# A grouped expert FFN with one list of 143 slot tiles, its tokens in parts of 16 and 16 tiles, and two more gate groups inside the second attention

## The chip, the cores and the metric

The kernel runs on one core of one Trainium2 chip. The metric is device time in microseconds (us). The core has five engines with queues of their own: PE multiplies matrices (its weight loads are shown as PEld), DVE and ACT do element work, POOL does element work and issues the indirect DMAs, and SP issues the plain DMAs.

## The reference

A transformer block works on 8 x 512 tokens of width 256 in float32:

```python
x = x + 0.5 * _L0_ffn_ref(_layernorm(x), ...)      # expert choice: 8 experts take 1024 tokens each
x = x + _L0_attn_ref(_layernorm(x), ...)           # causal, 16 heads of 16
x = x + 0.5 * _L0_ffn_ref(_layernorm(x), ...)
x = x + 0.5 * _L1_ffn_ref(_layernorm(x), ...)      # "FFN one" below
x = x + _L1_attn_ref(_layernorm(x), ...)           # 16 heads of 64: "the second attention"
x = x + 0.5 * _L1_ffn_ref(_layernorm(x), ...)      # "FFN two" below
```

The change is in the last three lines. In `_L1_ffn_ref` every token goes to 4 of 16 experts, and to a shared expert:

```python
scores = softmax(x @ gate_w.T)                     # 4 groups of 4 experts; the best 2 groups stay
_, indices = lax.top_k(masked, 4); weights = take(scores, indices)
h1 = einsum('td,edi->tei', x, w1); h3 = einsum('td,edi->tei', x, w3)
y = einsum('tei,eid,te->td', silu(h1) * h3, w2, c) # c holds the weights; 256 -> 128 -> 256 per expert
z = silu(x @ ws1) * (x @ ws3) @ ws2                # shared expert, inner width 256
return y + z
```

## The kernel before

The residual `x` stays on the chip as 32 tiles of 128 tokens; a group is 4 tiles. The engine queues are filled in the order in which the Python code emits (`manual_schedule`), so a waiting instruction holds up everything behind it on its engine.

**The grouped FFN** (`Grouped`, from L1220) sorts token rows by expert through DRAM. For each part of the tokens there is a list of slots, cut into slot tiles of 128 rows of which each belongs to one expert. `routing` (L1264) computes the gate on DVE for all tiles of a part: softmax, the best groups, the four best experts by repeated maxima, then with a few matmuls and scans the slot of every token (`self.slot`), the expert that owns each slot tile (`self.owner`) and the weights (`self.coef`). It is a generator: `advance(steps, n)` runs it n pieces further. `send` (L1245) copies each normalised row to its four slots with four indirect DMAs per token tile, issued by POOL; one is issued only when the one before the previous has landed (two in flight). `tile_steps` (L1498) works through the slot tiles two at a time, as a pipeline over steps: `turn` transposes a pair loaded by `load` four steps earlier, `hide` (L1532) is the first matmul and the silu two steps later, `back` a transpose, `give` (L1555) the second matmul and the write to `ys_d`. A load of a part waits for all sends of that part. `gather` (L1352) fetches the four result rows of each token of a tile with four indirect DMAs, again with a limited number in flight (`flying`), into one of two `yg` buffers, and `add` (L1366) adds them to `x`, weighted, on DVE. `collect` (L1374) lists steps "add tile t - 2, gather tile t", which the caller places between other work. `shared` (L1452) is the shared expert as units of PE and DVE work that a `Pump` deals out.

**Two parts.** `PARTS` is 12 and 20 tiles. Each part has a slot list of its own, of `slot_tiles(t)` tiles: 63 for 12 token tiles and 95 for 20, the most that 16 experts with a last tile filled in part can need. That makes 158 slot tiles in each FFN, worked in 80 pairs.

**FFN one** (`ffn1_before`, L1608) takes the parts in the order 12, 20. It normalises the first three groups, routes them beside units of the shared expert, sends their rows, then normalises and routes the other five groups beside more units, sends those rows, empties the pump, and runs the tile steps. Part 0's results are collected within the steps from step 37 on, one tile in three steps; at step 37 the 4 MB of attention weights are also loaded (`attn1_weights`, L894). Part 1's 20 tiles are collected inside the attention.

**The second attention** (`_attn1`, L912) is a loop over 64 chunks of two heads, of two halves each. Lists of small pieces are put between: the gathers of FFN one, layernorm statistics, and `Front` (from L1700), which computes the gate logits of FFN two for the groups whose tokens are finished (five groups, 20 tiles), routes them (from chunk 47 on) and sends their rows.

**FFN two** (`ffn1_after`, L1751) has the parts 20, 12. It loads the expert weights, normalises the last three groups and computes their logits on PE, then runs the tile steps with the routing of part 1 inside (four pieces a step), then the sends of part 1. Part 0 is collected in two steps of three from step 53 on, two gathers in flight. After the steps come the 48 units of the shared expert; every second unit is followed by one collect step of part 1, with four gathers in flight. `out` is written tile by tile.

Of the kernel before, what the change touches and what calls it, by code (L numbers as in the profile page):

```python
# [45 lines left out]
PARTS = 12, 20  # L46
# [9 lines left out]


def slot_tiles(t):

    return (t * P * TOPK + E1 * (P - 1)) // P  # L60


class Kernel:
    def __init__(self, ctx, tc, w):
# [59 lines left out]
        self.slots_d, self.ys_d = {}, {}  # L124
        for t in PARTS:
            self.slots_d[t] = self.dram.tile([slot_tiles(t) * P, D], F32, name=f"slots_d{t}")
            self.ys_d[t] = self.dram.tile([slot_tiles(t) * P, D], F32, name=f"ys_d{t}")

    def clear(self, zero, part, parts):

        for t in PARTS:
            rows = self.slots_d[t].rearrange("(j p) d -> p j d", p=P)
            a, b = slot_tiles(t) * part // parts, slot_tiles(t) * (part + 1) // parts
            self.nc.sync.dma_start(out=rows[:, a:b, :], in_=bc(zero, 1, b - a))
# [777 lines left out]
    def _attn1(self, ctx, weights, one, after):  # L912
# [185 lines left out]
        turned, sends = [], list(range(a))  # L1098
        flags = {"routed": False}
# [4 lines left out]
        def listed(n):  # L1104
            b, c = divmod(n, NC)
            got = gathered(n - 1) if 1 <= n <= one.parts[1] + 2 else []
            if c == 0:
                ranges = []
                if b == 0:
                    ranges.append((self.stats1, QT, 2 * QT))  # L1110
                elif 2 <= b < B - 1:
                    got += [each(means, self.stats1, (b + 1) * QT + i) for i in range(0, QT, 2)]
                    ranges.append((self.stats1, (b + 1) * QT, QT))
# [7 lines left out]
            if (b, c) == (groups, 4):  # L1121
                got += [each(means, after.stats, (b - 1) * QT + i) for i in range(0, QT, 2)]
                got += roots([(after.stats, (b - 1) * QT, QT)])
            return got

        def fill(n, half):
            b, c = divmod(n, NC)
            if half == 0:
# [3 lines left out]
                if c == 3 and 2 <= b <= groups or (b, c) == (groups, 6):  # L1132
                    got += turned.pop(0)
# [20 lines left out]
        for g in range(2 * N + 1):  # L1154
# [20 lines left out]
            if n < N:  # L1175
                scores(n, half)
                if half == 1 and (c == 2 and 2 <= b <= groups or (b, c) == (groups, 5)):
# [19 lines left out]
    def topk(self, pool, vals, n, k, hots):  # L1197
# [6 lines left out]
        for r in range(k):  # L1204
# [3 lines left out]
            rank = pool.tile([P, T, n], F32, name=f"rank{n}")  # L1208
# [11 lines left out]
class Grouped:  # L1220


    def __init__(self, k, n, parts):
        self.k, self.n, self.parts = k, n, parts
        self.base = (0, parts[0])
        self.tiles = [slot_tiles(t) for t in parts]
        self.slots_d = [k.slots_d[t] for t in parts]
        self.ys_d = [k.ys_d[t] for t in parts]
        late, most = k.late, max(parts)
# [4 lines left out]
        self.owner = [late.tile([1, slot_tiles(most)], I32, name=f"owner{h}") for h in range(2)]  # L1234
        self.stats = k.ln_tiles(late)
        self.sent, self.of_part = [], ([], [])
# [8 lines left out]
    def send(self, h, t, row):  # L1245

        nc, tc = self.k.nc, self.k.tc
        key = f"slots{self.n}{h}"
        for r in range(TOPK):
            inst = nc.gpsimd.indirect_dma_start(  # L1250
                out=self.slots_d[h][:, :],
                out_offset=bass.IndirectOffsetOnAxis(ap=self.slot[h][:, r, t : t + 1], axis=0),
                in_=row, in_offset=None,
                bounds_check=self.tiles[h] * P - 1, oob_is_err=True,
# [4 lines left out]
            tc.declare_no_dep(inst, group=key, keep=before, reason="slots of one part are all different")  # L1259
# [4 lines left out]
    def routing(self, h, lg, pool, row_psum):  # L1264
# [49 lines left out]
        tiles_i = pool.tile([P, E1], I32, name="tiles_i")  # L1314
        nc.vector.tensor_scalar(tiles_i, inc[:, :, HT - 1], float(P - 1), None, ALU.add)
        nc.vector.tensor_scalar(tiles_i, tiles_i, 7, None, ALU.arith_shift_right)
        nc.vector.tensor_tensor(inc.rearrange(flat), inc.rearrange(flat), pb, ALU.subtract)
        pa = row_psum(E1 * HT)
        nc.tensor.matmul(pa, lhsT=k.tri, rhs=chosen.rearrange(flat), start=True, stop=True)
        tiles = pool.tile([P, E1], F32, name="tiles")  # L1320
        nc.vector.tensor_copy(tiles, tiles_i)
        upto = pool.tile([P, E1], F32, name="upto")
        nc.vector.tensor_tensor_scan(upto, k.ones[:, 0:E1], tiles, 0.0, ALU.mult, ALU.add)
        base = pool.tile([P, E1], F32, name="base")
        nc.vector.tensor_tensor(base, upto, tiles, ALU.subtract)
        nc.vector.tensor_scalar(base, base, float(P), None, ALU.mult)
        nc.vector.tensor_tensor(inc.rearrange(flat), inc.rearrange(flat), pa, ALU.add)
        yield
        nc.vector.tensor_tensor(inc, inc, bc(base, 2, HT), ALU.add)
# [11 lines left out]
        past = pool.tile([P, E1], F32, name="past")  # L1341
        number = pool.tile([P, 1], F32, name="number")
        nc.vector.tensor_scalar(past, upto, k.lanes[:, 0:1], None, ALU.is_le, ALU.add, accum_out=number)  # L1343
# [8 lines left out]
    def gather(self, h, t, flying):  # L1352

        nc, tc = self.k.nc, self.k.tc
        y = self.y[h, t] = self.k.late.tile([P, TOPK, D], F32, name="yg", bufs=2)
        for r in range(TOPK):
            inst = nc.gpsimd.indirect_dma_start(  # L1357
                out=y[:, r, :], out_offset=None, in_=self.ys_d[h][:, :],
                in_offset=bass.IndirectOffsetOnAxis(ap=self.slot[h][:, r, t : t + 1], axis=0),
                bounds_check=self.tiles[h] * P - 1, oob_is_err=True,  # L1360
            ).ins
            for other in self.got[-flying : 1 - flying]:
                tc.add_manual_dep(inst, other.name, SYNC, reason="few transfers at a time")
            self.got.append(inst)

    def add(self, h, t, ranks=range(TOPK)):  # L1366
        at = self.base[h] + t
        x = self.k.x[:, at, :]
        for r in ranks:
            self.k.nc.vector.scalar_tensor_tensor(  # L1370
                x, self.y[h, t][:, r, :], self.coef[h][:, r, t : t + 1], x, ALU.mult, ALU.add
            )

    def collect(self, h, flying, then=None):  # L1374

        def step(t):
            def run():
                if t >= 2:
                    self.add(h, t - 2)
                    if then is not None:  # L1380
                        then(self.base[h] + t - 2)
                if t < self.parts[h]:
                    self.gather(h, t, flying)
            return run
        return [step(t) for t in range(self.parts[h] + 2)]
# [66 lines left out]
    def shared(self, g):  # L1452
# [4 lines left out]
        def hidden(s):  # L1457
# [14 lines left out]

            def dve():
# [4 lines left out]
        def outputs(i):  # L1478
# [11 lines left out]

            def dve():
# [6 lines left out]
    def tile_steps(self):  # L1498
# [3 lines left out]
        where = [(h, i, min(2, self.tiles[h] - i)) for h in range(2) for i in range(0, self.tiles[h], 2)]  # L1502
        st = [{} for _ in where]

# [410 lines left out]
```

## Time and profile before

| what | value |
|---|---|
| median of 3 runs | 4050.3 us (4047.67 to 4058.88) |
| the profiled execution | 4017.39 us, span 4015.7 us, mean granted PE clock 0.936 |
| FFN one: x has landed, first slot tile on PE, last result row of a slot tile | 1859.0, 2029.2, 2309.8 us |
| second attention: first transpose of it, last projection added to x | 2310.6, 3561.1 us |
| FFN two: first slot tile, first unit of the shared expert, end | 3581.1, 3895.7, 4015.7 us |
| PE, DVE, ACT, POOL busy, share of the span | 91%, 46%, 36%, 30% |

The times in the table are starts of instructions in the timeline of the profiled execution, in us from the start of the span. In the profile, L12 is line 12 of the kernel before; "x1264" is a number of instructions; "<-" after the bar names what ended most of the idle time before a group. In a table of windows the columns are the window, its length, the busy time of PE, PEld, DVE, ACT and POOL with the number of instructions, the granted PE clock, the busy share of the DMA engines and GB/s.

### The profile page before, as it was taken

The numbers are of one execution on the slowest core, as the hardware profiler recorded it, in microseconds if no ns is written. First come the engines' busy times: TensorE is split into PE (matmuls) and PEld (weight loads), VectorE is DVE, ScalarE is ACT, GpSimd is POOL, SyncE is SP. The second block draws the span as 40 slices with busy tenths as digits, with TensorE's granted clock in tenths as the row PEclk, the third lists the DMA queues.
The fourth block names the chain that finished last, engine by engine and source line by source line (L and its number), as shares of the span: only waits on it lengthen the run. The fifth ranks groups of instructions, "written<-read, shape, count | busy, mean of one in ns | idle before, by whom it ended". The sixth has DMA issues, their size and how long they took to land.

```text
span 4015.7 us, 52125 instructions
## 1 busy us (share of the span) xinstructions
PE 3662.2 (91%) x18444; PEld 2343.5 (58%) x18444; DVE 1858.5 (46%) x4396; ACT 1432.8 (36%) x2849; POOL 1203.8 (30%) x1074
## 2 busy tenths in 40 slices
PE   5799995999997599997798999999999999989978
PEld 5466662555556366665487845555555554558855
DVE  5312206555553421213733556666556576554444
ACT  2122221444443122222122355555455554533311
POOL 2233335334322133331553322220000004504254
PEclk6899997999986599998899999999999999989989
DMA  8533322010103033324256600110000001136543
GB/s 271 161 73 75 73 30 80 17 27 17 28 22 106 18 77 71 70 52 123 78 198 218 188 28 27 30 29 1 1 1 1 1 1 48 58 108 218 182 147 105
DMA packets 256141, 306.99 MB, mean 76 GB/s; under 512 B 34320, under 2 KB 225936, under 8 KB 255632
## 3 DMA queue, kind: packets, MB, share of 16 engines
q1 hardware_dynamic: 206736, 202.43, 15.8%
q0 software_dynamic: 49152, 101.24, 10.5%
q8 instruction: 153, 2.51, 0.3%
q14 instruction: 100, 0.82, 0.1%
HBM read 161.48 MB, written 133.69 MB: 74 GB/s over the span
## 4 chain that ended last, share of the span: by engine, by line
PE 41%; issue 4%; DVE 3%; DMA 3%; POOL 3%; ACT 1%; POOLq 0%; DVEq 0%; ACTq 0%; SPq 0%
PE sp L986 6%; PE tp L1006 6%; PE zp L1033 6%; PE pq L964 6%; PE hs L1537 4%; PE yp L1048 3%; PE pv L953 3%; PE yps L1559 2%; POOL slots_d L1250 2%; DMA yg<-ys_d,slot 2%; PE hp L1464 2%; POOL yg L1357 1%; PE tpx L1523 1%; DMA acc_d<-ob,idx 1%; PE rp L1020 1%
## 5 line engine op out<-in xcount | busy, mean ns | idle before, releaser
L478 PE MATMUL hp<-exT,w 128*128 128x512 f32 x1024 | 453.4, 597 | 0.0
L492 PE MATMUL op<-w,hid 128*128 128x256 f32 x2048 | 451.9, 380 | 0.0
L995 ACT ACTIVATE ex<-sp,nmax 128x512 f32<-128x512 f32 x512 | 344.7, 685 | 242.3 <-DVE nmax L992 242.3
L492 PEld LDWEIGHTS op<-w,hid 128*128 128x128 f32 x2048 | 387.7, 190 | 64.3 <-issue 15.3
L1357 POOL DMA_INDIRECT yg<-ys_d,slot x256 | 266.0, 1039 | 510.2 <-DVE x L1370 296.2
L497 DVE TENSOR_TENSOR ob<-op,b 128x256 f32<-128x256 f32 x128 | 54.4, 425 | 647.4 <-PE op L492 572.0
L731 DVE CUSTOM_DVE_ANT_0 junk<-sp,mask 128x128 f32<-128x128 f32 (+3 forms) x512 | 251.1, 490 | 198.0 <-PE sp L722 174.3
L499 POOL DMA_INDIRECT acc_d<-ob,idx x128 | 207.1, 1618 | 439.8 <-ACT ob L498 193.0
L992 DVE TENSOR_REDUCE nmax<-sp 128x2 f32<-128x1024 f32 x256 | 301.7, 1220 | 80.3 <-PE sp L986 80.2
L478 PEld LDWEIGHTS hp<-exT,w 128*128 128x128 f32 x1024 | 193.5, 191 | 219.9 <-issue 216.9
L1006 PEld LDWEIGHTS tp<-ident,ex 128*128 128x128 f32 x2048 | 234.4, 141 | 147.4 <-issue 86.6
L1537 PE MATMUL hs<-w_sb,xT 128*128 x1264 | 310.4, 390 | 2.5 <-DMA xs<-slots_d 1.3
L482 ACT ACTIVATE hid<-hp,b 128x512 f32<-128x512 f32 x256 | 175.9, 687 | 342.3 <-PE hp L478 342.3
L1006 PE MATMUL tp<-ident,ex 128*128 128x128 f32 x2048 | 272.5, 275 | 6.7 <-ACT ex L995 5.4
L1537 PEld LDWEIGHTS hs<-w_sb,xT 128*128 128x128 f32 x1264 | 248.4, 197 | 39.2 <-ACT xT L195 2.7
L1250 POOL DMA_INDIRECT slots_d<-wide,slot x176 | 174.4, 991 | 318.3 <-DVE past L1343 144.3
L986 PE MATMUL sp<-qk,qk 64*128 64x512 f32 x1024 | 254.4, 615 | 0.0
L964 PE MATMUL pq<-xnT,wide 128*128 128x512 f32 x512 | 247.5, 607 | 1.2 <-ACT xnT L195 0.8
L197 DVE COPY eT<-tp 128x512 f32<-128x512 f32 x256 | 176.9, 691 | 140.7 <-PE tp L1006 139.9
L1033 PE MATMUL zp<-eT,v 128*64 128x512 f32 x1024 | 236.0, 603 | 0.0
L195 ACT COPY eT<-tp 128x512 f32<-128x512 f32 x256 | 149.5, 584 | 240.4 <-PE tp L1006 240.4
L449 POOL DMA_INDIRECT ex<-xn_d,idx x128 | 131.3, 1025 | 345.9 <-DVE idx L440 311.8
(298 smaller groups left out, 5512.3 us busy)
## 6 DMA issues: line engine op xcount, KB each, us to landing
xs<-slots_d SPq DMA_DIRECT2D x156, 256.0 KB, 2.8
ys_d<-ys SPq DMA_DIRECT2D x156, 256.0 KB, 2.5
w<-in_W SPq DMA_DIRECT2D x32, 1024.0 KB, 6.1
w_sb<-in_w SPq DMA_DIRECT2D x24, 512.0 KB, 6.5
slots_d<-zero SPq DMA_DIRECT2D x7, 1536.0 KB, 12.9
xn_d<-xn SPq DMA_DIRECT2D x16, 512.0 KB, 4.2
acc_d<-x SPq DMA_DIRECT2D x8, 1024.0 KB, 5.7
x<-acc_d SPq DMA_DIRECT2D x8, 1024.0 KB, 9.5
```

What stands on the lines that cost most here:

```text
L478: nc.tensor.matmul(hp, lhsT=w1[:, c, f * P : f * P + P], rhs=exT[e][:, c, h * CH : h * CH + CH], start=(c == 0), stop=(c == DC - 1),)
L492: nc.tensor.matmul(op, lhsT=hid[h][:, f, i * P : i * P + P], rhs=w2[:, f, :], start=(f == 0), stop=(f == FC - 1),)
L731: nc.vector.tensor_tensor_reduce(out=junk[:, :wd], in0=sps[h // 2][:, h % 2, at : at + wd], in1=mask[:, S - wd :], scale=1.0, scalar=NEG, ...
L964: nc.tensor.matmul(pp, lhsT=(wq, wk)[a][:, k, c * P : c * P + P], rhs=xnT[b][:, k, :], start=(k == 0), stop=(k == DC - 1),)
L986: nc.tensor.matmul(sp[:, j, :], lhsT=q[r, qt * P : qt * P + P], rhs=k[r, :], start=True, stop=True)
L992: nc.vector.tensor_reduce(nmax, sp, AX.X, ALU.max, negate=True)
L995: nc.scalar.activation(ex[:, j, :], sp[:, j, :], AF.Exp, bias=nmax[:, j : j + 1], accum_out=ch["sums"][:, qt, j : j + 1],)
L1006: nc.tensor.transpose(tp[:, k, :], ch["ex", qt][:, j, k * P : k * P + P], self.ident)
L1033: nc.tensor.matmul(zp[DK1 * j : DK1 * j + DK1, :], lhsT=v[b, h][:, k, at : at + DK1], rhs=ch["eT"][:, j, k, :], start=(k == 0), stop=(k == ...
L1250: inst = nc.gpsimd.indirect_dma_start(out=self.slots_d[h][:, :], out_offset=bass.IndirectOffsetOnAxis(ap=self.slot[h][:, r, t : t + 1], ax ...
L1357: inst = nc.gpsimd.indirect_dma_start(out=y[:, r, :], out_offset=None, in_=self.ys_d[h][:, :], in_offset=bass.IndirectOffsetOnAxis(ap=self ...
L1537: nc.tensor.matmul(hp[:, u].rearrange("p a i -> p (a i)"), lhsT=st[j]["xT"][:, u, c, :], rhs=self.w13[:, bass.ds(st[j]["e"][u], 1), c, :]. ...
```

## The change

One list of `SLOT_TILES` = 143 slot tiles per FFN takes the place of two lists. Part 0 fills whole slot tiles from the front, as many as each expert has; the rows of an expert that are left over go to one of 16 tail tiles, which part 1's rows fill up before they go on. With parts of 16 and 16 tiles, FFN one works on the first 48 tiles (`starts`, `tiles`) as soon as part 0's rows are sent, and on the other 95 after part 1's; part 0's results are complete after tile 80 (`whole`). FFN two keeps 20 and 12: 64 tiles, 79 tiles, 96.

```diff
-PARTS = 12, 20
+PARTS = (16, 16), (20, 12)
+SLOT_TILES = (NT * TOPK + E1 * (P - 1)) // P
...
+        first = TOPK * parts[0] - E1
+        self.starts, self.tiles = (0, first), (first, SLOT_TILES - first)
+        self.whole = TOPK * parts[0] + E1
```

`routing` gets more instructions. For part 0, on arrays of 16 to 64 columns except the last three:

```diff
+            nc.vector.tensor_copy(tiles_i, count)
+            nc.vector.tensor_scalar(tiles_i, tiles_i, 7, None, ALU.arith_shift_right)
...
+            nc.vector.tensor_tensor(over, count, shift, ALU.add)
+            nc.vector.tensor_scalar(tail, each, full, float(P), ALU.add, ALU.mult)
+            nc.vector.tensor_scalar(at, upto, float(P), None, ALU.mult)
+            nc.vector.tensor_tensor(jump, tail, at, ALU.subtract)
...
+        nc.vector.tensor_tensor(inc, inc, bc(shift, 2, HT), ALU.add)
+        nc.vector.scalar_tensor_tensor(beyond, inc, 0.0, bc(jump, 2, HT), ALU.is_ge, ALU.mult)
+        yield
+        nc.vector.tensor_tensor(inc, inc, bc(at, 2, HT), ALU.add)
+        nc.vector.tensor_tensor(inc, inc, beyond, ALU.add)
```

Loads of part 0, sends of part 1, gathers of part 0 and writes of results behind tile 80 (96) are declared independent of each other. The four loads at the border of the parts are issued in the step that turns the first of them, not four steps ahead:

```diff
         def turn(j):
+            if j == early:
+                for ahead in range(4):
+                    load(j + ahead)
...
-            load(j + 4)
+            if j >= early or j + 4 < early:
+                load(j + 4)
...
-        first = sum(h == 0 for h, _, _ in where)
-        return load, step, len(where) + 4, first
+        known = sum(self.starts[h] + i < self.whole for h, i, _ in where)
+        return load, step, len(where) + 4, known
```

`collect` and `gather` get a mode `more`: four tiles in flight instead of two, every second one in two of the four `xs` buffers.

```diff
+        if more and t % 2:
+            halves = [self.work.tile([P, 2, D], F32, name="xs", bufs=4) for _ in range(2)]
+            y = [halves[r // 2][:, r % 2, :] for r in range(TOPK)]
...
+        depth = 4 if more else 2
```

The prelude of FFN one is a stream: `Pump.beside` runs three pieces of a generator before each hidden unit of the shared expert, one before each output unit, and four where no unit is left. The first four groups are normalised and their logits computed at the start; the other four are inside the second stream.

```diff
+    def beside(self, steps):
+        more = True
+        while more:
+            more = advance(steps, self.units[0][0].steps if self.units else 4)
+            self.run(1)
...
+        f.normal(3)
+        f.columns(3)
+        for g in (2, 3):
+            f.logits(g, lg, g * QT)
...
+        pump.beside(f.routing(0, lg, f.route, f.row_psum))
         for t in range(a):
             f.send(0, t, f.xn[:, t, :])
...
+        def second():
+            for g in range(a // QT, TT // QT):
+                for i in range(0, QT, 2):
+                    for t in range(g * QT + i, g * QT + i + 2):
+                        k.ln_mean(f.route, f.stats, t)
+                    yield
+                y = k.ln_root(f.route, f.stats, g * QT, QT)
+                yield
+                k.ln_rest(f.route, f.stats, g * QT, QT, y)
+                yield
+                f.normal(g)
+                yield
+                f.columns(g)
+                f.logits(g, lg, g * QT - a)
+                pump.feed(groups[g][0])
+                if g > a // QT:
+                    pump.feed(groups[g - 1][1])
+                yield
+            pump.feed(groups[-1][1])
+            yield from f.routing(1, lg, f.route, f.row_psum)
+        pump.beside(second())
         for t in range(f.parts[1]):
             f.send(1, t, f.xn[:, a + t, :])
...
-        begin, weights = first + 5, None
+        begin, weights = known + 5, None
...
-            if i >= begin and (i - begin) % 3 == 0 and coming:
+            if i >= begin and (i - begin) % 5 % 2 == 0 and coming:
                 coming.pop(0)()
```

In the attention, statistics, transposes and logits of groups 5 and 6 (tiles 20 to 27) are added at chunks 52 to 54 and 60 to 63; their logits go to a buffer `lg1`, and the routing there still covers the first 20 tiles.

```diff
+        later = {groups: 6, groups + 1: 6, groups + 2: 7}
...
-            if (b, c) == (groups, 4):
+            if b >= groups and c == 4:
...
-                if half == 1 and (c == 2 and 2 <= b <= groups or (b, c) == (groups, 5)):
+                if half == 1 and (c == 2 and 2 <= b <= groups or b >= groups and c == later[b] - 1):
                     turned.append(front.units(b - 2 if c == 2 else b - 1, row_psum))
```

FFN two then has one group left to normalise and gate before its steps. The routing runs three pieces a step, with two of the other groups' normalisations in the first two steps; part 0 is collected in three steps of five, and the rest is spread over all 48 units, with two gathers in flight throughout.

```diff
-        for g in range(a // QT, TT // QT):
-            f.normal(g)
-            f.columns(g)
-            f.logits(g, lg, g * QT - a)
-        steps = f.routing(1, lg, f.route, f.row_psum)
+        g = TT // QT - 1
+        k.ln_range(f.route, f.stats, g * QT, QT)
+        f.normal(g)
+        f.columns(g)
...
+        steps = f.routing(1, f.lg1, f.route, f.row_psum)
...
-                sending = not advance(steps, 4)
+                sending = not advance(steps, 3)
+                if i < 2:
+                    f.normal(rest.pop(0))
...
-            if i >= begin and (i - begin) % 3 != 2 and early:
+            if i >= begin and (i - begin) % 5 % 2 == 0 and early:
                 early.pop(0)()
-        last = f.collect(1, 4, done)
+        last = f.collect(1, 2, done, more=True)
...
+        ends = early + last
+        pace, at = len(ends) / len(pump.units), 0
         while pump.units or pump.pending:
             pump.run(1)
             at += 1
-            if at % 2 == 0 and early:
-                early.pop(0)()
-            elif at % 2 == 0 and last:
-                last.pop(0)()
+            if ends and len(early + last) - len(ends) < at * pace:
+                ends.pop(0)()
```

## The prediction

> **What bounds the kernel now.** I read the table of windows first, to see where PE is full, then the timelines of PE, POOL and DVE around the gaps.
>
> ```profile
> 1900.00:1940.00 40.00, 25.50 (x70) 14.90 (x69) 35.18 (x117) 4.07 (x7) 16.25 (x17) 0.78 0.14 51
> 2500.00:2700.00 200.00, 199.60 (x970) 112.04 (x970) 127.96 (x207) 105.67 (x250) 47.76 (x45) 1.00 0.09 27
> 3650.00:3700.00 50.00, 50.00 (x281) 44.60 (x280) 19.48 (x40) 17.03 (x39) 25.59 (x27) 1.00 0.71 235
> 3800.00:3850.00 50.00, 40.14 (x170) 32.90 (x169) 22.36 (x49) 10.47 (x23) 28.03 (x26) 0.81 0.57 171
> 3900.00:3950.00 50.00, 36.60 (x107) 19.68 (x105) 23.72 (x50) 5.25 (x9) 34.16 (x33) 0.93 0.35 100
> ```
>
> PE sets the pace in the attention (199.6 of 200 us) and in undisturbed slot-tile steps (50 of 50). It doesn't in FFN one's prelude, where DVE does the routing (35.2 of 40), nor where results are gathered (40.1 and 36.6 of 50). PE's timeline gives the price of a step, the same instruction one pair later, 3.25 us, and the stall where FFN one passes to its second part:
>
> ```profile
> 3653.82 1.03 PE L1559 MATMUL yps<-w_sb,aT 128*128 x4
> 3657.07 1.03 PE L1559 MATMUL yps<-w_sb,aT 128*128 x4
> ...
> 2137.22 1.11 PE L1523 MATMUL tpx<-ident,xs 128*128 128x128 f32 x4 [6.55 <-DMA xs<-slots_d]
> ```
>
> What PE waits for at 2137 is on POOL:
>
> ```profile
> 1917.33 1.03 POOL L1250 DMA_INDIRECT slots_d<-wide,slot  x1 [66.29 <-PE hp L1464]
> 1984.15 0.99 POOL L1250 DMA_INDIRECT slots_d<-wide,slot  x1 [0.30 <-issue]
> 2002.11 0.98 POOL L1250 DMA_INDIRECT slots_d<-wide,slot  x1 [16.97 <-DVE past L1343]
> 2131.63 0.98 POOL L1250 DMA_INDIRECT slots_d<-wide,slot  x1 [0.41 <-DMA slots_d<-wide,slot]
> ```
>
> The first 48 sends take 66.8 us (1.42 each, two in flight). The 80 of part 1 wait for the second routing and take 129.5 us: 1.70 each beside the steps' own loads and writes, about 1.38 without. The load follows the last, and PE goes on 5.6 us after its issue. The gathers of FFN two are on POOL too:
>
> ```profile
> 3763.31 1.07 POOL L1357 DMA_INDIRECT yg<-ys_d,slot  x1 [65.78 <-DMA ys_d<-ys]
> 3906.57 1.02 POOL L1357 DMA_INDIRECT yg<-ys_d,slot  x1 [1.20 <-DVE x L1370]
> ...
> 3917.98 1.02 POOL L1357 DMA_INDIRECT yg<-ys_d,slot  x1 [0.30 <-issue]
> 3919.31 1.02 POOL L1357 DMA_INDIRECT yg<-ys_d,slot  x1 [0.30 <-issue]
> ...
> 3980.06 1.02 POOL L1357 DMA_INDIRECT yg<-ys_d,slot  x1 [0.31 <-issue]
> ```
>
> Between the first two lines lie 19 tiles of four gathers: 7.54 us a tile with two in flight. With four in flight they leave every 1.33 us, 5.3 a tile. So the steps from 53 on are bound by two-in-flight gathers, and the end by what is left on PE after 3984.
>
> **Change: the tiles removed.** 158 slot tiles become 143, 80 pairs 72: 8 steps x 3.25 = 26 us per FFN where PE sets the pace. Whether they count depends on the chain of sends and gathers, so I follow that chain.
>
> **FFN one.** Part 0's slots were ready at 1916.4. Ahead of them now stand a fourth group's 8 transposes (2.15 us here), 16 gate matmuls (3.4) and four more tiles of statistics on DVE (4 x 0.53): +7.5, since each stands on the path in turn. Routing took 34.2 us for 12 tiles (1882.2 to 1916.4) and 38.9 for 20 (1963.2 to 2002.1); 16 tiles, 36.5. New are 7 small DVE instructions at 0.2 and three on 256 columns at 0.43, +2.8. So 1882.2 + 7.5 + 39.3 = 1929. Now 64 sends at 1.42: 2020. The second routing (the first's 39 us, plus four groups' statistics, rows and gates, 43 us for five groups before, 1920 to 1963) ends about 2008, under these sends, and costs nothing; without that cover each us late is a us lost. Steps begin at 2020 + 5.6 = 2026, against 2029. Part 1's 64 sends: 5 at 1.4, 38 beside the steps at 1.70, 21 at 1.38 once no loads are left, 101 us: 2121, and step 24 goes on at 2127. PE reaches it at 2026 + 24 x 3.25 = 2104, so it waits 23 us. Step 32 went on at 2137 before: a gain of 10.
>
> From there both versions have 48 pairs on PE. Before, these ended at 2310 with gathers at leisure (one tile in three steps). Now 16 tiles are to be gathered in 31 steps, three in five steps, 5.4 us a tile, faster than two in flight have ever gone here. First gather: 17.8 us after step 32 before, of which four steps are 13; now 20 steps + 4.8 = 70, 2197. The 4 MB of attention weights are loaded just then, as before, when the first eight gathers took 22 us, not 15: +7. Then 16 x 7.54 = 121, and 4 for landing and adding: 2329. PE alone would end at 2296: 2127 + 48 x 3.25, 8 for the pipeline's last four steps, 5 for the weights' traffic (PE busy 45 of 50 us there before). The attention waits on DVE behind the last add: it starts at 2330, not 2310.6, **+19**. Bounds: 6.4 us a tile (the quickest pairs there, 3.1 to 3.2 us) gives +1; 8 gives +26.
>
> **Attention.** Two more groups on a full PE: transposes 1.07 and gate matmuls 2.02 each, **+6** (up to +9, if DVE's share is felt). The 16 gathers fewer and the eight POOL normalisations of 1.22 us are hidden there; with a busier DVE they would cost up to 4.
>
> **FFN two, counted from the attention's end,** took 455 us. Two groups less before the steps: PE 2 x 5.64 = 11.3 us (from one group's transposes to the next's at 3563.87 and 3569.85, less overlap), so step 0 could start 12 us after the end, not 20. But the last 16 sends of part 0 now wait for the last gate group's transposes, some 28 us before the end, and run into the expert weights, which SP loads from 3542 at over 300 GB/s; beside FFN one's weights an indirect DMA took 3.3 us. Seven so and five at 1.42, then landing and load: step 0 at +16 (12 to 22). Routing on DVE took 32.6 us to the first send; new are 2.4 of instructions (as in FFN one, on fewer columns), 2.8 of two groups' rows and 3.9 for three steps more: 42. 48 sends took 82.8, +5.6, less 2 for quiet at their end: 86. So step 32, the new border, goes on at 16 + 42 + 86 = +144, where PE could be at about +130: a new stall of some 14, where the old border had none. First gather, 70 later: +214. Twelve tiles at 7.54 until the steps end: +304. The other 20 tiles (flying is now 2 for all) run beside the shared expert, 48 units and seven transposes, about 100 us on PE. No row shows this quiet a stretch with two in flight; bounds are 6.0 (twice the 2.7 us landing plus 0.3) and 7.54, the nearest row the last two tiles of the old phase, 3892.21 to 3906.57, 7.2. I take 6.8, since depth 4 frees the buffer earlier: 136, +440. Landing, last add and write: +447. **-8** (-24 to +7).
>
> *A rule against this.* The Trainium skill, "DMA: Bandwidth & Descriptors", section "Anatomy of one DMA — SWDGE (gpsimd) path", puts about 2.0 us of fixed, completion-bound cost on such a DMA, plus bytes / 436 GB/s: 2.3 us for 128 KB. The trace's gathers land after 2.9 (median). By the page's figure two in flight would keep up with POOL's 1.33 us, the 20 last tiles would take 106 us as an estimate, and the sum below would be 30 lower. I go by the rows.
>
> **Sum.** +19 + 6 - 8 = +17 on the profiled 4017.4, itself 33 us under the median of 4050.3 shown; I add the same us to the median: **4067**. The rest is hidden: `clear` writes 15 slot tiles less behind PE in the first FFN, SP issues fewer loads and writes.
>
> **Rivals.** (a) *Gathers go faster*, 6.0 to 6.4 us a tile everywhere. For it: those quick pairs, and PE's stalls thin the traffic. Against: 19 tiles held 7.54. At 6.4 FFN one loses 1 and FFN two gains 8 + 12 x 1.14 + 20 x 0.4 = 30: 1 + 6 - 30 = -23, 4027; at 6.0 the same sum is -6 + 6 - 42 = -42, 4008; say **4020**. It decides for faster from about 6.6 us a tile down. (b) *The border comes later still*: the second routing ends after the first 64 sends (statistics, roots, silu and DVE are dealt in one stream, with an ACT table load of 1.28 us at each change of function). From 2020 on each us is lost; ending at 2036 costs 16, **4083**. (c) *It cancels*: FFN one costs 10, FFN two gains 16, **4050**. (d) The independence that is declared doesn't hold, and part 0's gathers wait for all steps: over +90; nothing speaks for it.
>
> **Chances.** Forecast 0.50, alone 4052 to 4086; (a) 0.28; (b) 0.15; (c) 0.07, with (d) under 0.01. A measurement can't tell 0.3%, 12 us, from no change. Of the forecast's 0.50 I put 0.34 above 4062 and 0.16 within. Slower 0.34 + 0.15 = 0.49; same 0.16 + 0.07 = 0.23; faster 0.28. For 8 in 10 the range runs from the middle of (a), 4022, to past (b), 4092.
>
> **What would show it.** Right: PE idle some 20 us before step 24 of FFN one on `xs`, released by a send; POOL issuing sends without a pause from about 1930 to 2121; collects at 7 us a tile or more until the attention starts, later than 2320; a gap before step 32 of FFN two; gathers to within 10 us of the end. Wrong: steps of 3.25 us while gathers run, or an attention that starts before 2305.

## The result and the profile after

| | kernel before | changed kernel |
|---|---|---|
| median | 4054.1 us (4047.7 to 4058.9, 4 runs) | 4105.0 us (4101.4 to 4111.5, 4 runs) |
| profiled execution, span | 4015.7 us | 4104.5 us |
| FFN one's second routing ends, first slot tile on PE | 2001.8, 2029.2 | 2077.1, 2080.5 |
| second attention, first and last PE work | 2310.6, 3560.7 | 2393.4, 3653.6 |
| FFN two, from the attention's end: first slot tile, first gather, end | 20, 203, 455 | 12, 208, 451 |

The ratio is 1.0128, 95% interval 1.0107 to 1.015: slower, as forecast (4067), but by 51 us and above the range (4022 to 4092). The profile shown of before is of an execution of 4017.4 us, faster than all four of its runs here. The table of windows after, first three windows of FFN one's prelude, then stretches that answer to those shown of before:

```profile
1920.00:1940.00 20.00, 18.74 (x58) 10.60 (x58) 10.81 (x35) 6.32 (x8) 14.04 (x14) 0.76 0.25 86
1940.00:1980.00 40.00, 13.51 (x41) 9.92 (x42) 7.81 (x29) 1.38 (x3) 29.32 (x30) 0.59 0.28 99
1980.00:2010.00 30.00, 5.53 (x8) 1.96 (x6) 0.00 (x0) 0.00 (x0) 19.80 (x21) 0.56 0.27 92
...
2500.00:2700.00 200.00, 200.00 (x932) 105.88 (x929) 125.92 (x180) 101.91 (x246) 46.87 (x45) 1.00 0.10 30
...
3800.00:3850.00 50.00, 50.00 (x278) 44.43 (x277) 18.54 (x38) 16.67 (x39) 0.00 (x0) 1.00 0.53 164
...
3900.00:3950.00 50.00, 42.04 (x181) 32.94 (x180) 24.11 (x53) 12.47 (x28) 29.02 (x28) 0.86 0.51 155
3950.00:4000.00 50.00, 26.87 (x73) 13.54 (x72) 19.73 (x42) 4.06 (x7) 31.86 (x30) 0.81 0.27 77
```

From 1940 to 2010 little but POOL works: PE has 19 us of work in 70, DVE 8 and ACT 1.4, and after 1980 DVE and ACT do nothing. The later stages look as predicted: PE full in the attention and in steps without gathers, and far from full where results are gathered. The timeline of POOL, the three places at FFN one's sends:

```profile
1920.87 1.03 POOL L1250 DMA_INDIRECT slots_d<-wide,slot  x1 [79.16 <-DVE past L1378]
...
2006.25 0.98 POOL L1250 DMA_INDIRECT slots_d<-wide,slot  x1 [0.34 <-issue]
2077.40 0.98 POOL L1250 DMA_INDIRECT slots_d<-wide,slot  x1 [70.17 <-DVE slot L1372]
```

64 sends leave without a pause, one every 1.35 us; then POOL waits 70.17 us for the second routing, which was to end under them. What holds that routing up is seen on PE and ACT, the engines of its chain (timelines of the same stretch):

```profile
1951.22 1.92 PE L1491 MATMUL tp<-ident,wide 128*128 128x128 f32 x8
1969.86 0.61 PE L1499 MATMUL lg<-gw,xnT 128*128 128x16 f32 x2 [16.73 <-issue]
1976.15 3.17 PE L1499 MATMUL lg<-gw,xnT 128*128 128x16 f32 x14 [5.68 <-issue]
1979.16 6.36 PE L1520 MATMUL hp<-xnT,ws_sb 128*128 128x512 f32 x8
2013.28 3.78 PE L1520 MATMUL hp<-xnT,ws_sb 128*128 128x512 f32 x4 [27.75 <-ACT sg L1526]
```

```profile
1969.22 0.59 ACT L1494 COPY xnT<-tp 128x512 f32<-128x512 f32 x1 [24.58 <-remote]
1975.52 0.59 ACT L1494 COPY xnT<-tp 128x512 f32<-128x512 f32 x1 [5.71 <-remote]
2011.34 1.28 ACT L1526 ACT_TABLE_LOAD   x1 [35.23 <-remote]
```

PE's eight transposes are drawn as done at 1953.1, but ACT can copy the first four only at 1969.2; the `hp` product is drawn as done at 1985.5, and ACT's silu starts with its table load at 2011.3. "remote" is a release that the view can put down to no instruction, and the ends of PE's bars are modelled. The times of PE's semaphore updates, which the trace also holds, tell how late they are:

```
transposes, modelled ends        1951.6 1951.9 1952.1 1952.3 1953.1
hp (two products), modelled ends 1982.9 1985.5
PE semaphore updates             1955.2 1961.5 1963.6 1965.7 1967.8 1969.2 1975.5 2011.27 2011.33
```

Taken in order, the nine updates are two of the product before, five of the transposes and two of `hp`; so the last transpose's is 22 us behind its modelled end, and those of `hp` are 28 and 26. PE's completions reach the others ever later while the sends run, and the last two arrive together just after the sends end. The stream is one chain through PE, ACT and DVE, so each late completion holds up all three. After that the stream runs at its own speed, and everything later is shifted by the 65 to 70 us.

PE's timeline at the border of the parts, and POOL's first gather, after:

```profile
2186.49 1.11 PE L1592 MATMUL tpx<-ident,xs 128*128 128x128 f32 x4 [31.19 <-DMA xs<-slots_d]
```

```profile
2256.83 1.06 POOL L1407 DMA_INDIRECT yg<-ys_d,slot  x1 [74.71 <-DMA ys_d<-ys]
```

The prediction had this stall, at 23 us in place of 31, and this distance, 70 us. Its sum went wrong before this point.

### The profile page after: what moved, and what is told of

Its sections match the earlier page's. It is cut to its first block, busy times and chain, and to the rows that moved or that the text cites. A ratio compares the mean times of both kernels' runs of the same rounds, so it can differ in the third digit from the quotient of the medians.

```text
span 4104.5 us, 51324 instructions
## 1 busy us (share of the span) xinstructions
PE 3632.8 (89%) x18190; PEld 2305.5 (56%) x18190; DVE 1851.5 (45%) x4427; ACT 1430.2 (35%) x2823; POOL 1216.9 (30%) x1082
## 4 chain that ended last, share of the span: by engine, by line
PE 57%; issue 10%; POOL 7%; DMA 6%; DVE 5%; ACT 2%; SPq 0%; POOLq 0%; DVEq 0%; ACTq 0%
PE sp L979 6%; PE tp L999 6%; PE pq L957 6%; PE zp L1026 5%; PE hp L471 5%; PE op L485 5%; POOL slots_d L1250 4%; PE pv L946 3%; PE yp L1041 2%; DMA yg<-ys_d,slot 2%; PE st L760 2%; POOL yg L1407 2%; PE hs L1607 2%; PE z L774 2%; PE sp L715 2%
## 5 line engine op out<-in xcount | busy, mean ns | idle before, releaser
L1407 POOL DMA_INDIRECT yg<-ys_d,slot x232 | 244.3, 1053 | 525.0 <-DVE x L1424 262.8
L1607 PE MATMUL hs<-w_sb,xT 128*128 x1144 | 285.9, 395 | 1.8 <-DMA xs<-slots_d 0.7
L1607 PEld LDWEIGHTS hs<-w_sb,xT 128*128 128x128 f32 x1144 | 227.7, 200 | 37.3 <-ACT sgs L1613 1.2
```

Of the source, the lines that this page charges most:

```text
L1407: inst = nc.gpsimd.indirect_dma_start(out=y[r], out_offset=None, in_=self.k.ys_d[:rows, :], in_offset=bass.IndirectOffsetOnAxis(ap=self.sl ...
L1607: nc.tensor.matmul(hp[:, u].rearrange("p a i -> p (a i)"), lhsT=st[j]["xT"][:, u, c, :], rhs=self.w13[:, bass.ds(st[j]["e"][u], 1), c, :]. ...
```

## Experiments

The first theory was that the change itself makes the 70 us: either the sends make PE late (A), or the stream, the chain through PE, ACT and DVE that leads to the second routing, is slow by itself (B). Edits below are of the changed kernel unless said otherwise; the letters in the expectations (A to I) are explained where they first stand.

**1. The same program on another chip.** Meant to take the sends out of the stream's way:

```diff
-        for t in range(a):
-            f.send(0, t, f.xn[:, t, :])
...
         pump.beside(second())
+        for t in range(a):
+            f.send(0, t, f.xn[:, t, :])
```

> The changed kernel, with the 64 sends of FFN one's part 0 issued only after the second routing's stream, so that nothing is sent while that stream runs. Theory A (TensorE's matmuls complete late as long as these sends run beside them): without sends the stream runs at its own speed and the second routing ends some 80 us after the first, near 2000 instead of 2077; the part 0 sends then take 86 us, the steps begin near 2092, and the time stays at 4105 to 4120, but the stall of PE and ACT is gone from the trace. Theory B (the stream is slow by itself, a chain DVE, ACT, PE with a table load at each change of function): the second routing still ends near 2077, the sends come on top, and the time is about 4185.

The edit did nothing to the program that runs (it is "run 1" below): POOL's queue has only these sends here, so the order in which the program names them and other engines' work doesn't count. Every engine's queue holds the same instructions in the same order as in the changed kernel. And yet the time was 4040.0 us, beside 4021.2 for the kernel before. Windows, then POOL:

```profile
1940.00:1980.00 40.00, 33.73 (x129) 19.95 (x128) 19.00 (x68) 14.23 (x19) 28.65 (x30) 0.91 0.28 96
1980.00:2010.00 30.00, 24.71 (x76) 13.31 (x74) 24.45 (x67) 3.67 (x5) 19.54 (x20) 1.00 0.27 93
```

```profile
2006.84 0.98 POOL L1250 DMA_INDIRECT slots_d<-wide,slot  x1 [0.89 <-DMA slots_d<-wide,slot]
2012.25 0.98 POOL L1250 DMA_INDIRECT slots_d<-wide,slot  x1 [4.42 <-DVE slot L1372]
```

PE works 58 of these 70 us, not 19, and the routing costs POOL a wait of 4.4 us. So the 65 us aren't in the instructions: the chip, or the state that it is in, decides. Two more runs on this chip, with statistics in one block and with four gathers in flight at the end, show no lateness either.

> The changed kernel, with the statistics of groups 4 to 7 (means, one square root over 16 tiles) made in one block ahead of the second stream, so that the stream has no square roots between its silus. Theory A (completions late beside the sends): the stall stays, the second routing ends after the last send, time 4095 to 4110. Theory B (table loads and the chain of DVE, ACT and PE for each group's statistics): the routing ends near 2010, and the time falls by 60 to 70 us, to about 4040.

Time 4038.8, beside 4040.0 for run 1. That this is near what theory B expected proves nothing: on this chip there was no lateness to take away. The routing ends 13 us earlier (1999.2), still under the sends (last at 2008.9): its cover is real, and what the stream saves counts for nothing.

The unedited kernel was then timed on three chips.

> The changed kernel itself, nothing edited, beside new runs of the kernel before. In the profile of the result the second stream of FFN one stood still from 1936 to 2011; in the last runs, of which one left this stage in effect as it was (POOL does not follow the order in which the program names sends and other engines' work), it did not. Theory A (the change costs 70 us there): the ratio to before is again 1.0128, about +51 us, with the stall in the profile. Theory D (the stall is not of the change; by its own work it costs what the run without it showed, 4038.3 - 4019.5 in span): ratio 1.0045 to 1.005, +18 to +20 us, the second routing over near 2000, the attention starting near 2327 and no gap in the part 1 sends.

> The changed kernel itself once more. The chips met so far are of two kinds: on two the kernel before took 4016 to 4021 and PE did not fall behind; on one (and in the first result) it took 4050 to 4055 and PE did. Theory G: on a chip of the first kind the change costs what its own work costs, 18 to 24 us, ratio 1.0045 to 1.006; on one of the second kind 1.0105 to 1.013 as before, with PE behind from about 1936 to 2011. Theory A: 1.0105 to 1.013 on either.

> The changed kernel itself, beside the former. Theory G: on a chip of the first kind ratio 1.0045 to 1.006 (4040 against 4021, as in the one look at its instructions there), on one of the second kind 1.0105 to 1.013. Theory A: 1.0105 to 1.013 on either.

Ratios 1.0105 (1.0074 to 1.0136), 1.0124 (1.01 to 1.0148) and 1.0141 (1.0119 to 1.0163), beside 4054.7, 4055.3 and 4045.0 for the kernel before, and each time the same picture: part 1's first send at 2079.2, 2078.8 and 2077.8. On each of these three chips the lateness repeats. The chip of run 1 doesn't have it, nor does one more met below, where the kernel before took 4016.0.

**2. What makes PE late.** First the order of the second stream, on one of the chips with the lateness: the blocks of the kernel before in its place (an earlier version of this run gave no result).

```diff
-        pump.beside(second())
+        k.ln_range(f.route, f.stats, a, 8)
+        pump.run(2)
+        f.normal(4)
+        f.normal(5)
...
+        steps = f.routing(1, lg, f.route, f.row_psum)
```

> The changed kernel, with the work on groups 4 to 7 and the second routing written in the block order of the kernel before in place of the stream. Where the stream does not stall, its routing is over under the part 0 sends in either order (1998 in the run with block statistics), so FFN one changes by less than 5 us and the time is that of the unedited kernel. If the order costs anything, it shows as a gap in POOL's sends between part 0 and part 1.

4087.8: from the last send of part 0 to the first of part 1 it is 55.6 us, not 72.3 as in the unedited kernel on this chip, so the gap shrinks but stays. The order of the stream is worth 17 us of it.

Then four on the same chip: the kernel before itself, and three edits of the sends.

> The kernel before itself, profiled beside its new runs. Theory G (on the chips where both kernels are slower, PE's completions fall behind while POOL issues indirect transfers every 1.3 to 1.4 us without a pause and little else moves; this costs the kernel before too): if the time is near 4054, PE stands in the same stage, while 48 sends run from 1917 to 1984, and perhaps again while its last gathers leave every 1.33 us, and the 33 us over the first profile of it (4017.4) lie there. Theory A (the stall belongs to the change alone): no such stall, the 33 us are spread over all stages or lie in the first layers. If the time is near 4020, the chip is one of those without the stall, and the run shows none.

It took 4047.3. Its windows in the same stage:

```profile
1940.00:1960.00 20.00, 18.59 (x72) 12.95 (x70) 4.34 (x11) 3.64 (x5) 14.57 (x15) 0.75 0.27 98
1960.00:1980.00 20.00, 5.90 (x27) 5.50 (x27) 0.69 (x1) 2.75 (x5) 11.82 (x12) 0.51 0.32 109
```

PE falls behind here too, but later and only until its 48 sends end at 1975. From first to second routing it took 113.8 us, against 85.4 in the profile shown of before: 28.5 lost. FFN two, where four gathers in flight leave every 1.33 us at the end, took 466.4 against 455.0: 11.4 more, with a hole of 9.4 us in the gathers where DVE's add comes late. The first routing came 8 us earlier, which no edit explains, so the span is 30 us longer. That is most of the distance between the first profile (4017.4) and the medians. POOL's timeline, at the sends and at the hole:

```profile
1974.83 0.98 POOL L1250 DMA_INDIRECT slots_d<-wide,slot  x1 [0.33 <-issue]
2022.35 0.98 POOL L1250 DMA_INDIRECT slots_d<-wide,slot  x1 [46.54 <-DVE past L1343]
...
3994.15 1.02 POOL L1357 DMA_INDIRECT yg<-ys_d,slot  x1 [9.42 <-DVE x L1370]
```

Pacing, by a fill of 0.33 us on POOL after each send:

```diff
+        pad = f.route.tile([P, 256], F32, name="pad")
         for t in range(a):
-            f.send(0, t, f.xn[:, t, :])
+            f.send(0, t, f.xn[:, t, :], pad)
...
+            if pad is not None:
+                nc.gpsimd.memset(pad, 0.0)
```

> The changed kernel with a small fill of a tile on POOL after each of FFN one's part 0 sends, so that they leave every 1.7 us or more, not every 1.34. Theory G: with pauses PE completes in time, the second routing ends near 2005 to 2010, part 0's sends end near 2030 to 2040, part 1's follow at once, and on a chip with the stall the time falls by 35 to 45 us to about 4062; on one without, it rises by 0 to 20 from about 4040. Theory H (any send beside this stream delays PE, whatever the pace): the second routing ends 60 to 70 us after the last send, later than now, and the time rises by 20 us or more to about 4125.

```profile
1931.89 0.33 POOL L1265 MEMSET pad<- 128x256 f32 x1
1932.38 0.98 POOL L1250 DMA_INDIRECT slots_d<-wide,slot  x1 [0.17 <-issue]
1933.36 0.34 POOL L1265 MEMSET pad<- 128x256 f32 x1
1933.86 0.98 POOL L1250 DMA_INDIRECT slots_d<-wide,slot  x1 [0.16 <-issue]
```

```profile
1940.00:1980.00 40.00, 34.41 (x127) 20.65 (x126) 19.67 (x67) 14.51 (x20) 34.08 (x53) 0.87 0.25 85
1980.00:2010.00 30.00, 24.96 (x76) 14.09 (x74) 24.73 (x67) 3.50 (x5) 25.62 (x39) 0.96 0.25 86
```

The first fence is POOL's timeline, the second the windows: sends every 1.48 us (1.55 on average), PE busy 59 of 70 us, the routing over at 2012.2, exactly as in run 1, and 4041.6 us. A tenth to a seventh more time between sends takes the whole lateness away; 1.7 us, as expected, wasn't needed. This is one execution, but it repeats on the two other chips with the lateness: from 1940 to 2010 PE is busy 17, 19 and 19 us in the unedited kernel on the three, and 59, 62 and 59 us in `paced`, `best2` and `best3`, whose sends have this fill.

Holding the sends for real, by a dependence:

```diff
         pump.beside(second())
+        nc.vector.tensor_copy(f.slot[0][:, :, :a], f.slot[0][:, :, :a])
         for t in range(a):
             f.send(0, t, f.xn[:, t, :])
```

> The changed kernel with part 0's sends of FFN one truly held: DVE copies their slot numbers onto themselves after the second routing, so no send leaves before. Theories G and H: PE runs the stream at its own speed, the second routing ends near 2000; then 128 sends, the first slot tile near 2092, and the time is 4100 to 4120 on either kind of chip. Theory B (the stream is slow by itself): the routing ends near 2077 without any send beside it, and the time passes 4170.

4120.6. Without any send beside it the routing ends at 2009.3, and PE works 56 of the 70 us. So theory B falls: on the same chip the stream isn't slow by itself.

Spreading SP's weight loads among the sends, one to five:

```diff
+            for n, inst in enumerate(made):
+                self.k.tc.add_manual_dep(inst, self.sent[n * every].name, SYNC, reason="one load to a few sends")
```

> The changed kernel with the 12 loads of FFN one's expert weights (6 MB) not ahead of the routing but one to every fifth send of part 0, so that SP's queue moves data through most of the stage. Theory G with quiet queues as its cause: beside this traffic PE completes in time, as it does when part 1's sends run beside slot-tile loads; the sends take longer, 64 at 1.7 or 109 us, the routing ends under them near 2010, and on a chip with the stall the time falls by 30 to 40 us to about 4068. If the pace of the sends alone decides: the sends slow to 1.7 near each load and the gain is about the same, but PE falls behind again between the loads. Theory H: no gain, 4105 to 4130.

4058.7: sends every 1.78 us, no lateness, routing over at 2018.6. The loads slow the sends, so this doesn't tell traffic from pace; the pace alone would explain it. Theory H falls with these runs: beside slower sends PE is in time.

Over several executions, the pacing on the changed kernel and on the kernel before (with a fill after its last gathers too):

> The kernel of the run with a fill of 128x256 on POOL after each part 0 send of FFN one, timed in rounds. Theory G: on a chip where the kernel before takes some 4050, PE does not fall behind, time 4035 to 4048, ratio 0.995 to 0.999; on one where it takes some 4020, there is no stall to take away, time 4035 to 4048 too, ratio 1.003 to 1.006. Theory I (the one look was luck, the stall comes and goes): some of the executions near 4105.

> The kernel before with the same pacing: a fill of 128x240 on POOL after each part 0 send of FFN one and after each gather of FFN two's last collect. It takes the stall away from the kernel before, so that the change can be judged without it. Theory G: time 4022 to 4030 on a chip with the stall (4050 without the fill), ratio 0.993 to 0.995, and the change by itself costs about what the prediction's sum said, paced5 minus oldp 13 to 20 us. Theory A: nothing changes, ratio 1.

This chip was of the kind without the lateness: 4045.8, ratio 1.0073 (1.0059 to 1.0086), and 4027.5, ratio 1.0022 (1.001 to 1.0034), beside 4016.0. There is nothing to cure, and the fill costs a little. The two paced kernels differ by 18.3 us, the unpaced ones beside run 1 by 18.8. That these agree shows little: the fills stand in different places, and in the kernel before they cost 11.5 us, mostly at the last gathers (FFN two 465.8 us in place of 455.0). That the fill gives the kernel before its 30 us back on the other kind of chip was not measured.

**3. Gathers.**

```diff
-        last = f.collect(1, 2, done, more=True)
+        last = f.collect(1, 4, done, more=True)
```

> The changed kernel with four gathers of FFN two's last 16 tiles in flight in place of two. If the two in flight bound the end, as the prediction had it (6.8 us a tile against 5.3 at 1.33 us each), the last 16 tiles take 85 us instead of about 110, and the time falls by 15 to 25 us to about 4085. If the end is bound by the shared expert's units on PE and DVE, which the gathers are dealt beside, nothing changes: 4100 to 4110.

On the chip of run 1: 4026.2. FFN two ends 424.2 us after the attention, 25 earlier than in run 1; the time falls by 14 alone, since here the first send of FFN one left 9.5 us later. It is part 1's 12 tiles that gain (the expectation wrongly speaks of 16): 5.5 us a tile against 7.2.

> The changed kernel with four gathers in flight in place of two in all three collects (FFN one's part 0, FFN two's part 0 and part 1). Theory E (two in flight bound the collects: 8.2 us a tile in FFN one, 6.8 at the end): FFN one's 16 tiles go at 6 to 6.5 us, the attention starts 25 to 30 us earlier, near 2300, FFN two ends 30 us earlier than with two, and the time is 35 to 40 us under before, ratio near 0.990. Theory F (beside slot-tile steps the gathers are bound by DMA traffic and by the adds that free their two buffers, not by the number in flight): FFN one unchanged, only the end gains its 26 us, ratio near 0.998.

All collects with four in flight, on a chip with the lateness: 4096.3, ratio 1.009 (1.0061 to 1.0119). FFN one's collect falls from 8.4 to 7.4 us a tile, between what the two theories said. But at the end, after 32 gathers without a pause, POOL stands still:

```profile
4013.60 1.03 POOL L1407 DMA_INDIRECT xs<-ys_d,slot  x1 [0.30 <-issue]
4034.36 1.02 POOL L1407 DMA_INDIRECT yg<-ys_d,slot  x1 [19.74 <-DVE x L1424]
```

DVE's add, which frees a buffer, stands behind shared-expert work. DVE's timeline in that stretch:

```profile
4005.88 0.69 DVE L1533 TENSOR_TENSOR at<-sg,hp 128x512 f32<-128x512 f32 x1 [10.86 <-remote]
4017.16 0.69 DVE L1533 TENSOR_TENSOR at<-sg,hp 128x512 f32<-128x512 f32 x1 [10.59 <-remote]
```

"remote" again, on products of PE: the same lateness, now beside gathers every 1.33 us. Paced sends, four in flight, and the fill after FFN two's gathers (best) and FFN one's too (best3):

```diff
-        coming = f.collect(0, 2, ready)
+        coming = f.collect(0, 4, ready, pad=pad)
...
-        early = f.collect(0, 2, done)
+        early = f.collect(0, 4, done, pad=pad)
...
-        last = f.collect(1, 2, done, more=True)
+        last = f.collect(1, 4, done, more=True, pad=pad)
```

> The paced kernel, with four gathers in flight in place of two in all collects, and the same fill after each gather of FFN two so that they leave every 1.48 us and not every 1.33. Expected from the runs so far: FFN one's collect 7.4 us a tile in place of 8.3, 14 us; FFN two's last 16 to 20 tiles at 5.9 to 6.0 in place of 6.8, 16 to 18 us: time 4008 to 4015, ratio to before 0.989 to 0.992. If the fill is not enough beside the shared expert (theory H), PE falls behind in the last 100 us as it did with four in flight and no fill (a 20 us hole in the gathers there), and the time is 4025 to 4035.

> The paced kernel with four gathers in flight, as run before at 0.9934. On a chip of the first kind again 0.992 to 0.995. On one of the second kind the kernel before is some 33 us slower and this one, if its fills keep PE from falling behind everywhere, is not: 3990 to 4000, ratio 0.985 to 0.988; if four gathers in flight still hold PE up there, 4005 to 4020, ratio 0.989 to 0.993.

> The paced kernel with four gathers in flight, with the fill after FFN one's gathers too. On a chip of the first kind nothing to gain: FFN one's collect 6.6 to 6.8 us a tile, ratio 0.992 to 0.995. On one of the second kind: if it was the unpaced gathers that took 7.8 us a tile there and not 6.6, they take 6.7 now, and the time falls by 15 us against the run without this fill (4011) to about 3996, ratio 0.984 to 0.987; if that was PE's lateness from other traffic, 0.987 to 0.991 again.

| run | chip | time | ratio to before |
|---|---|---|---|
| best | without lateness | 3990.6 | 0.9934 (0.9922 to 0.9947) |
| best2, the same kernel | with | 4010.9 | 0.9892 (0.987 to 0.9914) |
| best3 | with | 3997.0 | 0.9885 (0.9866 to 0.9903) |

The first was better in time than its expectation: FFN one took 6.6 us a tile, not 7.4 (its ratio was worse, since the kernel before took 4016.0 there). On the other kind of chip this was 7.8, so best2 lies where its expectation has PE still held up by the gathers; with the last fill it was 7.0, not the 6.7 expected. What this fill is worth in time isn't shown: best2 and best3 ran on different chips, and their ratios overlap. These versions beat both kernels on either kind of chip.

## Why the prediction was wrong

**The step that failed** is this one of FFN one: the second routing "ends about 2008, under these sends, and costs nothing". By its instructions it nearly does: 2012.0 in run 1, 2009.3 in "held". In the result it ended at 2077, because PE, on which that cover rests, completes late beside sends that leave every 1.35 us. The prediction took PE's pace under the sends from the one profile of before, an execution in which PE kept its pace. Of its own signs, the sends without a pause to 2121 failed by a pause of 70 us; the others came true. Rival (b) had the place and the rule (from 2020 on each us is lost) but priced the stream's own work, and gave 16 us to what cost 65.

**The second slip** was to add "the same us to the median". The 33 us between the profile and the medians shown were no constant: most of them were this same lateness in the kernel before, 28.5 us beside its 48 sends and 11.4 at its last gathers. The change sends 64 times in place of 48, and gives the lateness 85 us to grow in place of 66. The profile was of an execution without it, and the medians fit executions with it; the gap was there to see, and wasn't asked about. That "slower" came true is in part luck: of the 51 us about a third is what the sum was made of.

**The rest of the sum held in the main.** Measured on run 1, where these steps can be seen without the lateness:

| term | predicted | run 1 |
|---|---|---|
| part 0's sends, first to last | 1929 to 2020 | 1919 to 2007 |
| first slot tile, step 24 goes on | 2026, 2127 | 2015, 2123 |
| first gather, us a tile, attention starts | 2197, 7.5, 2330 | 2193, 8.2, 2327 |
| attention, longer by | 6 | 12 |
| FFN two: step 0, first send, step 32, first gather, end | 16, 58, 144, 214, 447 | 13, 50, 138, 209, 449 |

- FFN one, +19: +16. The gathers were slower than priced and the routing before them quicker; that these nearly cancel is luck.
- Attention, +6: +12. The two groups' transposes and gates were sized right (PE 6.1 us more); other transposes took 2.9 more and PE's waits 2.8. The bound of 9 was too low.
- FFN two, -8: -6. The steps begin 8 us earlier than before, PE waits at the new border, and the last 20 tiles take 7.0 us each (6.8 taken).
- Sum +17: the three terms, measured against the profile shown of before, give +22. In time run 1 is 18.8 over the kernel before on that chip, one execution of each. Rival (a), quicker gathers, fell: 8.2 us a tile, not 6.4. And 15 slot tiles fewer gain little where sends and gathers set the pace, as the text said.

**The rule weighed there.** The Trainium skill, "DMA: Bandwidth & Descriptors", section "Anatomy of one DMA — SWDGE (gpsimd) path", would by its cost of 2.0 us plus bytes / 436 GB/s let two in flight keep up with POOL's 1.33 us. The runs disagree: 7.2 us a tile with two in flight at the end, 5.5 with four; the gathers of run 1 land after 2.9 us (median).

## What to carry to other kernels

When a profile and the medians beside it differ by more than they scatter, find out what the difference is before you add a change to either. Work that is hidden under a stream of transfers is hidden only if the engines under it keep their pace there: look at when others are released, not at where a matmul's bar ends. An indirect-transfer stream that isn't the bound can be spaced out a little, and the number in flight chosen apart from the pace; where nothing was late, the fills cost the kernel before 11.5 us.

## What was not expected of the hardware

- The same instructions took 4040 us on one chip and about 4103 on three others, and the kernel before 4016 to 4021 and 4045 to 4055. The difference lies almost wholly where POOL issues indirect DMAs every 1.33 to 1.40 us and PE works beside them; at 1.48 to 1.55 it is gone. Part 1's sends, at 1.6 us beside slot-tile steps, don't delay PE: it is busy 49.4 of 50 us there, in the result too.
- On the chips with the lateness every trace also lacks records: 150 to 219 of PE's some 3500 semaphore updates, and 18 to 31% of the DMA landings; on the others none. The paced runs lack them too, but counted in the stage of the 64 sends the loss goes with the lateness: of their 1024 landing records (16 a send) the result's trace has 225, `paced` 865, and `held`, where nothing else works beside the sends, 1024, as run 1. Yet part 1's sends lose records (1080 landings of all queues in that stretch, 1677 in run 1) and PE isn't late there. So the loss alone doesn't make PE late; why its completions arrive late, and whether the taking of the profile has a part in it, stays open; no run told them apart.
